# One PSUM bank for the two query-tile pairs of an attention step, three bias transposes in one tile, and four tiles of x loaded in head 14

## The chip, the cores and the metric

The kernel runs on one core of a Trainium2 chip. The metric is the device time of one execution in microseconds (us), lower is better. Three runs of the kernel before gave a median of 2459.82 us (2456.49 to 2463.15).

The engines are called as the profile calls them: PE is TensorE (matmuls; PEld is its loading of weights), DVE is VectorE, ACT is ScalarE, POOL is GpSimd, SP is SyncE, which here only issues DMAs. Each engine works through its own queue in order; semaphores tie the queues together. PSUM is the memory that PE writes into. [...]DVE and ACT read it.

## The reference

One block of a transformer with adaptive layer norm, all float32: 2048 tokens, model width 512.

```
mod = (silu(c) @ wmod)                      # sa, ca, ga, sb, cb, gb
h = layernorm(x) * (1 + ca) + sa
q = h Q_w + Q_b;  k = h K_w + K_b;  v = h V_w + V_b      # 16 heads of 128
scores = softmax(causal(q k^T / sqrt(128)))
x = x + ga * (concat_heads(scores v) O_w + O_b)
h = layernorm(x) * (1 + cb) + sb
x = x + gb * (experts(h) + shared(h))       # 64 experts of width 128, top 4; 2 shared of width 512
```

The change touches only the first half: the start (biases), the attention of the 16 heads, and the handing over to the output projection.

## The kernel before

**Start.** x is loaded in four blocks of 512 tokens, normalised on DVE (`norm_x`), transposed on PE (`turn_x`) and written by ACT, scaled, into `hT` (`place_x`). In between, at L375 to L379, the three bias matrices (16 heads x 128) are transposed on PE into PSUM tiles `bps` and copied by DVE into `qkb`. Each of the three has a tile of its own with the tag "po", of which there are two buffers. So the third transpose waits until DVE has copied the first.

**Attention.** For each head there are 16 query tiles of 128 rows, taken in pairs pr = 0 to 7 (256 query columns). Five steps s = 0 to 4 make a head:

```
BATCHES = ((7,), (6,), (5, 0), (4, 1), (3, 2))
```

Steps 0 and 1 hold one pair, steps 2, 3 and 4 two. The causal mask gives pair pr 2 pr + 2 key tiles. The loop at L736 runs over all 80 steps; in step n it weaves three streams of PE work together (`merge`, L83, which gives the streams turns in proportion to their columns):

- the softmax of step n + 2 (`softmax_tile`): scores by PE into `ps` (L497), the mask and the row maximum by DVE (L509, L510), exp by ACT (L516), and the division by the row sum, on DVE for s < 2 (L484), on ACT as `p<-p,rs` for the others (L704);
- the weighted values of step n (`weighted_values`): for each pair 2 pr + 2 matmuls into one PSUM tile `po` (L569), then one copy by ACT that adds the bias of V, `at<-po` (L578), then one DMA from POOL's queue that writes `at` to the DRAM tensor `atd` (L581);
- fillers: the projections of the next head's q and k (L217, steps 0 to 2) or the next pair of heads' v (L424, steps 3 and 4), and near the end the first output projections (`begin_output`, L678).

Between softmax and weighted values the probabilities must be transposed. After step n's streams `swap(n + 2)` issues 16 DMAs on SP that exchange blocks of 32 partitions from `p` to `pt` (L541, some 10 us of issue). One step later DVE transposes within the blocks, in two halves (`turn`, L551), at 0.55 and 0.8 of the step's columns. So a `po` matmul of step n + 2 needs both halves.

**Buffers that the change touches.** PSUM tiles with the tag "po" have two buffers of one bank each. A pair takes one, half filled (256 of 512 columns). The banks therefore rotate by pairs: 7, 6, 5, 0, 4, 1, 3, 2, and a pair waits until ACT has copied the pair two places before it. `at` has two buffers of 256 columns, and a copy into it waits until the DMA two places before has read it.

**The end of attention.** From head 14 on the weights of the output projection (`load_wo`), parts of `atd` (`load_ab`, L659), four tiles of x (`load_x_tile`, L668) and O_b (L770) are loaded by SP. Tiles 0 and 1 of x are loaded in head 14, step 4; tiles 2 and 3 in head 15, step 2, after `load_ab(2)`, four DMAs that make up 2 MB. All four tiles take buffers of the pool `ktp`, which otherwise holds the k of the heads (6 buffers); `qtp` does the same for q. `begin_output(t)` sums the heads 0 to 14 of token tile t on PE, then DVE adds the x tile (L688) and the bias (L689). At head 15, step 4, SP loads the first 512 tokens of head 15 from `atd` again (L783, L784); after the last step the pools of attention are given up, their memory is used by the next stage, and the output projection (L1027, L1048), the second layer norm (L862 to L873), routing and experts follow.

Of the kernel before, what the change touches and what calls it, by code (L numbers as in the profile page):

```python
# [9 lines left out]
F32 = mybir.dt.float32  # L10
BF16 = mybir.dt.bfloat16
U32 = mybir.dt.uint32
AF = mybir.ActivationFunctionType
ALU = mybir.AluOpType
# [4 lines left out]
P = 128  # L19
# [4 lines left out]
def adaln_block_kernel(  # L24
# [23 lines left out]
    nc = tc.nc  # L48
    _, N, D = x.shape
    H, _, DH = Q_w.shape  # L50
# [12 lines left out]
    scale = 1.0 / math.sqrt(DH)  # L63
# [4 lines left out]
    ident = const.tile([P, P], F32)  # L68
# [10 lines left out]
    atd = dram.tile([H, DH, N], F32)  # L79
# [39 lines left out]
    NE = 4  # L119
    parts = [silc.rearrange("p k n -> p (k n)")]  # L120
    with ExitStack() as att:
        enter = att.enter_context
# [139 lines left out]
        with tc.tile_pool(name="pre", bufs=1) as pre, tc.manual_schedule():  # L262
# [3 lines left out]
            b16s = []  # L266
# [62 lines left out]
            def norm_x(b):  # L329
                mv = pre.tile([P, 4, 2], F32, name="mv", bufs=2)  # L330
                for i in range(4):
                    st = pre.tile([P, 6], F32, name="st", bufs=4)
                    nc.vector.bn_stats(st, xs[b][:, i, :])
                    nc.vector.bn_aggr(mv[:, i, :], st)
                rstd = pre.tile([P, 4], F32, name="rstd", bufs=2)
                nc.scalar.activation(rstd, mv[:, :, 1], AF.Sqrt, bias=eps, scale=1.0)
                nc.vector.reciprocal(rstd, rstd)
                for i in range(4):
                    nc.vector.tensor_scalar(
                        xs[b][:, i, :], xs[b][:, i, :], mv[:, i, 0:1], rstd[:, i : i + 1],  # L340
                        ALU.subtract, ALU.mult,
                    )
# [29 lines left out]
            place_x(0, 0)  # L372
            place_x(0, 1)
            norm_x(1)
            for b in range(3):  # L375
                bps = psA.tile([P, H], F32, name="bps", tag="po")
                nc.tensor.transpose(bps, b16s[b], ident[:H, :H])
                nc.vector.tensor_scalar(qkb[:, b, :], bps, scale if b == 0 else 1.0, None, ALU.mult)
            nc.vector.tensor_sub(qkb[:, 3, :], qkb[:, 1, :], qkb[:, 0, :])  # L379
            for b in range(1, NB):  # L380
                for half in range(2):
# [13 lines left out]

        pp = enter(tc.tile_pool(name="pp", bufs=2))
        ptp = enter(tc.tile_pool(name="ptp", bufs=2))
        atp = enter(tc.tile_pool(name="atp", bufs=2))
        smp = enter(tc.tile_pool(name="smp", bufs=6))
        PW = 4 * (4 * NP - 1) * 32  # L400

# [151 lines left out]
        def weighted_values(hd, s, pt):  # L553

            g, hh = divmod(hd, HG)
            RB = blocks_of(s)
            rows = pt[:, : 4 * RB * 32].rearrange("k (a r q) -> k r a q", a=4, q=32)
            out = []
            for pr in BATCHES[s]:
                last = 2 * pr + 1  # L560
                box = []

                def one(kt, pr=pr, last=last, box=box):
                    if kt == 0:
                        box.append(psA.tile([P, 2 * P], F32, name="po", tag="po"))
                    po = box[0]
                    r = first_block(s, pr) + kt
                    wide = kt < last
                    nc.tensor.matmul(  # L569
                        out=po if wide else po[:, P:],  # L570
                        lhsT=vts[g, kt // 4][:, kt % 4, hh * DH : (hh + 1) * DH],
                        rhs=rows[:, r : r + last + 1 : last] if wide else rows[:, r + last],
                        start=(kt == 0),
                        stop=(kt == last),
                    )
                    if kt == last:
                        at = atp.tile([P, 2 * P], F32, name="at")
                        nc.scalar.activation(  # L578
                            at, po, AF.Identity, bias=qkb[:, 2, hd : hd + 1], scale=1.0
                        )  # L580
                        nc.gpsimd.dma_start(out=atd[hd, :, pr * 256 : (pr + 1) * 256], in_=at)  # L581

                for kt in range(last + 1):
                    out.append((256 if kt < last else 128, lambda kt=kt, one=one: one(kt)))
            return out
# [78 lines left out]
        xts = {}  # L664

        def load_x_tile(t):
            xts[t] = ktp.tile([P, 512], F32, name="kt")
            nc.sync.dma_start(out=xts[t], in_=x[0, t * P : (t + 1) * P, :])  # L668

        def begin_output(t):  # L670
# [54 lines left out]
        with tc.manual_schedule():  # L725
            work = softmax_work(0) + softmax_work(1)
            fill = [(1024, lambda t=t: make_v(0, t)) for t in range(NT)]
            fill += [(2048, lambda j=j: plain(0, j, qts[0, j])) for j in (2, 0, 1)]
            merge([work[:4], fill[:8]], [])
            swap(0)  # L730
            merge([work[4:], fill[8:]], [])
            swap(1)
            turn(0, 0)
            turn(0, 1)
            outs = []
            for n, (hd, s) in enumerate(steps):  # L736
                if s == 3:
                    if hd + 2 < H:
                        heads[hd + 2] = load_head(hd + 2)
                    if hd % HG == 1 and hd // HG + 2 < NG:  # L740
                        groups[hd // HG + 2] = load_group(hd // HG + 2)
                fill = fillers(hd, s)
                if (hd, s) in MOD_LOADS:
                    load_mod(MOD_LOADS[hd, s], hd // HG)
                if (hd, s) in MOD_ROWS:
                    fill.append((2048, lambda m=MOD_ROWS[hd, s]: late_mod(*m)))
                if (hd, s) in ((2, 3), (6, 3)):
                    mag = qkw.tile([P, 512], F32, name="p_")
                    gate(mag, ga if hd == 2 else gb)
                if (hd, s) == (14, 1):  # L750
                    fill.insert(2, (0, lambda: load_wo(0)))
                if (hd, s) == (14, 2):
                    load_wo(1)
                    load_ab(0, heads=((0, 4), (4, 8)))
                if (hd, s) == (14, 3):
                    load_wo(2)
                    load_ab(0, heads=((8, 12), (12, 14)))
                    first, second = [
                        vow.tile([P, DC, HG, DH], F32, name="wv").rearrange("p k i d -> p (k i d)")
                        for _ in range(2)  # L760
                    ]
                    parts += [first[:, :D], first[:, D:], second[:, :D]]
                    last3 = second[:, D : D + (NE - 1) * P]
                if (hd, s) == (14, 4):
                    load_wo(3)
                    load_ab(0, heads=((14, 15),))
                    load_x_tile(0)
                    load_x_tile(1)
                    rest = spare(hd // HG)
                    nc.sync.dma_start(out=rest[0][:, :D], in_=O_b.partition_broadcast(P))  # L770
                    for u in range(NE):
                        outs += begin_output(u)
                if hd == H - 1 and s == 0:
                    load_ab(1, heads=((0, 4), (4, 8)))
                if hd == H - 1 and s == 1:
                    load_ab(1, heads=((8, 12), (12, 15)))
                if hd == H - 1 and s == 2:
                    load_ab(2)
                    load_x_tile(2)
                    load_x_tile(3)  # L780
                if hd == H - 1 and s == 4:
                    nc.vector.tensor_copy(ga, rest[0][:, D:])
                    nc.sync.dma_start(out=last3, in_=atd[H - 1, :, : (NE - 1) * P])  # L783
                    nc.sync.dma_start(out=ones, in_=atd[H - 1, :, (NE - 1) * P : NE * P])  # L784
                if outs:
                    upto = 8 if hd < H - 1 else (14, 14, 14, 10)[s]
                    fill += outs[:upto]
                    del outs[:upto]
                streams = [weighted_values(hd, s, turned.pop(n)), fill]
                if n + 2 < len(steps):  # L790
                    streams.insert(0, softmax_work(n + 2))
                marks = [(f, lambda i=i: scale_wo(i)) for f, i in WO_SCALES.get((hd, s), ())]
                if s == 4 and hd + 2 < H:
                    marks.append((0.3, lambda: sum_w(hd + 2)))
                if n + 1 < len(steps):
                    marks.append((0.55, lambda: turn(n + 1, 0)))
                    marks.append((0.8, lambda: turn(n + 1, 1)))
                merge([st for st in streams if st], marks)
                if n + 2 < len(steps):
                    swap(n + 2)  # L800
            assert not outs and not ahead
# [676 lines left out]
```

## Time and profile before

| | us |
|---|---|
| median of three runs | 2459.82 |
| the profiled execution, its own time | 2473.66 |
| its span, first to last instruction | 2471.9 |
| mean granted PE clock | 0.991 of full |
| ACT copies `at<-po` L578 | 128 x 0.462 |
| POOL issues `atd<-at` L581 | 128, 0.627 each on average, 128 KB each |
| DVE copies of the biases L378 | 3 x 0.167 |
| ACT copy 128x512 from PSUM, L225 | 0.67 to 0.68 |

In the rows of groups of instructions the profile names the line, the engine, the operation and the tiles as output<-input, then the busy time and how long one takes. The bracket at the end of a row of the timeline is the time that the engine stood idle before the instruction, and what released it. A row of the waits reads "who <- for whom: us in total, times, longest". The clock column is the share of the full PE clock that was granted: 0.50 means that matmuls take twice as long. Times in the timeline count from the span's start.

The stages by the timeline: the first po matmul starts at 113.5 us, the last at 1729.5; a head takes about 100 us and a step about 20.

### The profile page before, as it was taken

What the parts mean: (1) busy time and instruction counts of PE and PEld (TensorE: products, weight loads), DVE (VectorE), ACT (ScalarE), POOL (GpSimd) and SP (SyncE); (2) the same over time, 40 slices, a digit from 0 to 9 for tenths busy, and PEclk for the clock granted to TensorE, in tenths of its full rate; (3) what the DMA queues carried; (4) which work ended last, traced back from release to release, by engine and by line L of the source; (5) the groups of instructions that cost most, each with busy time, mean ns of one, the idle gap of its engine ahead of it and who ended that gap; (6) DMA issues with size and microseconds to landing.
All of it is one profiled execution on the core that took longest, in us unless ns stands there. A gap on an engine that the chain in (4) does not pass through costs nothing. (4 is left out here: it accounts for less than half of the span.)

```text
span 2471.9 us, 26333 instructions
## 1 busy us (share of the span) xinstructions
PE 2376.8 (96%) x8406; PEld 1504.6 (61%) x8406; DVE 1512.2 (61%) x2878; ACT 838.1 (34%) x1785; POOL 224.1 (9%) x286
## 2 busy tenths in 40 slices
PE   7999999999999999999999999998999999999989
PEld 3656656566565665666656656555444476877734
DVE  5367666676666766667667676663655563644654
ACT  3244443443444434444344444432111222222200
POOL 0000000000000000000000000000000011111163
PEclk9999999999999999999999999999999999999989
DMA  4234444454354443444445444564432378778564
GB/s 137 62 79 113 116 118 106 97 135 107 94 133 104 101 119 91 111 111 104 116 96 122 105 103 118 161 174 128 152 119 85 102 206 249 230 212 252 171 190 133
DMA packets 223682, 325.23 MB, mean 132 GB/s; under 512 B 31876, under 2 KB 138424, under 8 KB 223544
## 3 DMA queue, kind: packets, MB, share of 16 engines
q1 hardware_dynamic: 196664, 252.21, 39.5%
q0 software_dynamic: 17664, 54.54, 7.3%
q10 hardware_dynamic: 9216, 16.78, 1.8%
q8 instruction: 68, 1.11, 0.2%
q14 instruction: 70, 0.57, 0.1%
HBM read 138.86 MB, written 41.94 MB: 73 GB/s over the span
## 5 line engine op out<-in xcount | busy, mean ns | idle before, releaser
L516 ACT ACTIVATE p<-ps,nm 128x1024 f32<-128x1024 f32 (+7 forms) x384 | 332.2, 865 | 897.0 <-DVE nm L514 411.5
L569 PE MATMUL po<-pt,v 128*128 128x256 f32 (+1 forms) x2304 | 575.5, 369 | 38.4 <-ACT at L578 33.4
L569 PEld LDWEIGHTS po<-pt,v 128*128 128x128 f32 x2304 | 426.5, 191 | 288.2 <-issue 190.5
L497 PE MATMUL ps<-kt,qt 128*128 128x512 f32 (+3 forms) x1280 | 531.2, 531 | 19.2 <-ACT p L516 16.8
L510 DVE TENSOR_REDUCE nm<-ps 128x1 f32<-128x1024 f32 (+7 forms) x384 | 348.8, 908 | 56.6 <-PE ps L497 47.8
L551 DVE STREAM_TRANSPOSE pt<-pt 128x1664 f32<-128x1664 f32 (+2 forms) x160 | 317.9, 1987 | 44.1 <-DMA pt<-p 40.5
L497 PEld LDWEIGHTS ps<-kt,qt 128*128 128x128 f32 x1280 | 234.7, 190 | 179.2 <-issue 137.0
L424 PE MATMUL pv<-wv,hT 128*128 128x256 f32 x1024 | 240.8, 379 | 2.2 <-ACT v L431 2.2
L581 POOL DMA_DIRECT2D atd<-at x128 | 80.1, 627 | 1649.4 <-ACT at L578 1111.7
L424 PEld LDWEIGHTS pv<-wv,hT 128*128 128x128 f32 x1024 | 194.4, 190 | 31.2 <-ACT v L431 3.0
L704 ACT ACTIVATE p<-p,rs 128x1024 f32<-128x1024 f32 (+7 forms) x256 | 200.0, 805 | 6.2 <-DVE rs L472 5.8
L509 DVE TENSOR_TENSOR ps<-ps,causal 128x128 f32<-128x128 f32 x256 | 74.1, 289 | 176.9 <-PE ps L497 174.5
L1048 PE MATMUL pso<-hT,T 128*128 128x512 f32 x384 | 175.6, 602 | 0.0
L217 PE MATMUL pqk<-T,sw 128*128 128x512 f32 x360 | 169.2, 592 | 0.0
L1340 PE MATMUL pse<-wgu,xbT 128*128 128x256 f32 x512 | 121.1, 379 | 0.0
L1048 PEld LDWEIGHTS pso<-hT,T 128*128 128x128 f32 x384 | 70.3, 193 | 72.1 <-issue 71.3
L217 PE MATMUL pqk<-hT,wq 128*128 128x512 f32 x240 | 113.7, 596 | 0.0
L1257 PE MATMUL psd<-wsd,hs 128*128 128x512 f32 x256 | 111.5, 592 | 0.0
L1340 PEld LDWEIGHTS pse<-wgu,xbT 128*128 128x128 f32 x512 | 93.8, 190 | 11.7 <-issue 1.0
L217 PEld LDWEIGHTS pqk<-T,sw 128*128 128x128 f32 x360 | 68.4, 190 | 47.7 <-issue 43.0
L1323 POOL DMA_INDIRECT xb<-h2d,tok x64 | 65.1, 1018 | 302.2 <-PE tpx L1333 273.0
L1335 ACT COPY xbT<-tpx 128x512 f32<-128x512 f32 x64 | 37.4, 586 | 145.7 <-DVE y L1363 58.0
(364 smaller groups left out, 2364.9 us busy)
## 6 DMA issues: line engine op xcount, KB each, us to landing
pt<-p SPq DMA_DIRECT2D x768, 104.0 KB
pt<-p SPq DMA_DIRECT2D x256, 124.0 KB
pt<-p SPq DMA_DIRECT2D x256, 108.0 KB
atd<-at POOLq DMA_DIRECT2D x128, 128.0 KB
wgu<-in_L_ffn_Wg_dram SPq DMA_DIRECT2D x64, 256.0 KB
wgu<-in_L_ffn_Wu_dram SPq DMA_DIRECT2D x64, 256.0 KB
wd<-in_L_ffn_Wd_dram SPq DMA_DIRECT2D x64, 256.0 KB
ybd<-y ACTq DMA_DIRECT2D x64, 256.0 KB
```

The lines of the kernel that those rows point to most:

```text
L217: nc.tensor.matmul(out=ps, lhsT=l[:, k], rhs=r[:, k], start=(k == 0), stop=(k == 1))
L424: nc.tensor.matmul(out=ps, lhsT=hTs[t // 4][:, k, (t % 4) * P : (t % 4 + 1) * P], rhs=wv[:, k].rearrange("p i d -> p (i d)"), start=(k == ...
L497: nc.tensor.matmul(out=ps[:, o : o + wo], lhsT=q, rhs=kts[hd, (c0 + o) // 512][:, :wo], start=True, stop=True,)
L510: nc.vector.tensor_reduce(nm[:, n : n + 1], ps[:, :w], AX.X, ALU.max, negate=True)
L516: nc.scalar.activation(rows[:, r0 + c0 // P : r0 + (c0 + w) // P], ps[:, :w].rearrange("q (r b k) -> q r b k", b=4, k=32), AF.Exp, bias=nm ...
L551: nc.vector.transpose(part, part)
L569: nc.tensor.matmul(out=po if wide else po[:, P:], lhsT=vts[g, kt // 4][:, kt % 4, hh * DH : (hh + 1) * DH], rhs=rows[:, r : r + last + 1 : ...
L581: nc.gpsimd.dma_start(out=atd[hd, :, pr * 256 : (pr + 1) * 256], in_=at)
L704: nc.scalar.activation(part, part, AF.Identity, scale=r)
L1048: nc.tensor.matmul(out=ps, lhsT=abs_[pr][:, hd, i * P : (i + 1) * P], rhs=wos[hd // 4][:, hd % 4, :], start=(hd == 0), stop=(hd == H - 1),)
L1257: nc.tensor.matmul(out=ps, lhsT=hsh[b, f][:, i * P : (i + 1) * P], rhs=wsd[:, f, :], start=(f == 0), stop=(f == NHC - 1),)
L1340: nc.tensor.matmul(out=ps, lhsT=xts[e][:, k, :], rhs=weights[e][:, k].rearrange("p i h -> p (i h)"), start=(k == 0), stop=(k == DC - 1),)
```

## The change

Three edits:

1. In `weighted_values` one PSUM tile `po` of a whole bank (2 x 256 columns) is taken per step. Pair n of the step accumulates into its half n. There is one ACT copy per step, after the last matmul of the last pair, of one or both halves; then one DMA per pair, in order. `at` becomes a single buffer of 2 x 256 columns; its size in memory is the same.
2. The three bias transposes write into one tile `bps`; the three copies by DVE come after all of them.
3. The four tiles of x are loaded together in head 14, step 4, before O_b. Tiles 2 and 3 take buffers of `qtp` instead of `ktp`. Nothing of x is loaded in head 15 any more.

```
+            bps = psA.tile([P, 3, H], F32, name="bps", tag="po")
             for b in range(3):
-                bps = psA.tile([P, H], F32, name="bps", tag="po")
-                nc.tensor.transpose(bps, b16s[b], ident[:H, :H])
-                nc.vector.tensor_scalar(qkb[:, b, :], bps, scale if b == 0 else 1.0, None, ALU.mult)
+                nc.tensor.transpose(bps[:, b], b16s[b], ident[:H, :H])
+            for b in range(3):
+                nc.vector.tensor_scalar(
+                    qkb[:, b, :], bps[:, b], scale if b == 0 else 1.0, None, ALU.mult
+                )
...
-        atp = enter(tc.tile_pool(name="atp", bufs=2))
+        atp = enter(tc.tile_pool(name="atp", bufs=1))
...
-            for pr in BATCHES[s]:
+            box = []
+            for n, pr in enumerate(BATCHES[s]):
                 last = 2 * pr + 1
-                box = []
-
-                def one(kt, pr=pr, last=last, box=box):
-                    if kt == 0:
-                        box.append(psA.tile([P, 2 * P], F32, name="po", tag="po"))
-                    po = box[0]
+
+                def one(kt, n=n, pr=pr, last=last):
+                    if not box:
+                        box.append(psA.tile([P, 2, 2 * P], F32, name="po", tag="po"))
+                    po = box[0][:, n]
...
-                    if kt == last:
-                        at = atp.tile([P, 2 * P], F32, name="at")
+                    if kt == last and n == len(BATCHES[s]) - 1:
+                        at = atp.tile([P, 2, 2 * P], F32, name="at")
                         nc.scalar.activation(
-                            at, po, AF.Identity, bias=qkb[:, 2, hd : hd + 1], scale=1.0
+                            at[:, : n + 1], box[0][:, : n + 1], AF.Identity,
+                            bias=qkb[:, 2, hd : hd + 1], scale=1.0,
                         )
-                        nc.gpsimd.dma_start(out=atd[hd, :, pr * 256 : (pr + 1) * 256], in_=at)
+                        for m, o in enumerate(BATCHES[s]):
+                            nc.gpsimd.dma_start(
+                                out=atd[hd, :, o * 256 : (o + 1) * 256], in_=at[:, m]
+                            )
...
         def load_x_tile(t):
-            xts[t] = ktp.tile([P, 512], F32, name="kt")
+            if t < 2:
+                xts[t] = ktp.tile([P, 512], F32, name="kt")
+            else:
+                xts[t] = qtp.tile([P, 512], F32, name="qt")
...
                 if (hd, s) == (14, 4):
...
-                    load_x_tile(0)
-                    load_x_tile(1)
+                    for u in range(NE):
+                        load_x_tile(u)
...
                 if hd == H - 1 and s == 2:
                     load_ab(2)
-                    load_x_tile(2)
-                    load_x_tile(3)
```

## The prediction on record

> **What bounds the kernel now.** I read the page's busy shares first, then the stages, then TensorE's (PE's) waits, and last the instructions around them. The first line below is from the page, the others from the windows view, cut before the first attention step, at its end, and around one late stall.
>
> ```profile
> PE 2376.8 (96%) x8406; PEld 1504.6 (61%) x8406; DVE 1512.2 (61%) x2878; ACT 838.1 (34%) x1785; POOL 224.1 (9%) x286
> ```
>
> ```profile
> 113.00:1735.00 1622.00, 1567.60 (x5446) 1008.31 (x5447) 1060.36 (x1843) 669.80 (x1416) 80.09 (x128) 1.00 0.46 114
> 1735.00:2472.00 737.00, 717.67 (x2633) 440.88 (x2631) 395.07 (x916) 131.29 (x300) 142.96 (x150) 0.98 0.57 175
> 1592.80:1596.20 3.40, 3.40 (x6) 1.68 (x6) 0.00 (x0) 1.86 (x4) 1.07 (x2) 0.50 0.55 153
> 1707.00:1712.20 5.20, 5.09 (x8) 2.86 (x9) 0.00 (x0) 1.14 (x3) 1.07 (x2) 0.50 0.57 150
> ```
>
> The columns are the stretch, its length, busy time of PE, PEld, DVE (VectorE), ACT (ScalarE) and POOL, then the granted PE clock. In the attention stage (113 to 1735) PE is busy 1567.6 of 1622 us; no other engine passes 66%. Time can be won only from PE's 54 idle us and from its slow-clock stretches. PE's waits in that stage:
>
> ```profile
> PE po L569 <- ACT at L578: 33.4, 16, 6.9
> PE ps L497 <- ACT p L516: 16.8, 16, 1.6
> PE po L569 <- DVE pt L551: 3.6, 1, 3.6
> ```
>
> Total us, times, longest. The first row is two thirds of it, once per head. The timeline shows where, in one head: PE first, then ACT.
>
> ```profile
> 477.98 1.88 PE L497 MATMUL ps<-kt,qt 128*128 128x512 f32 x4
> 481.68 0.70 PE L569 MATMUL po<-pt,v 128*128 128x256 f32 x2 [1.81 <-ACT at L578]
> ```
>
> ```profile
> 480.24 1.03 ACT L704 ACTIVATE p<-p,rs 128x896 f32<-128x896 f32 x1
> 481.17 0.83 ACT L578 ACTIVATE at<-po,qkb 128x256 f32<-128x256 f32 x2
> 481.88 0.83 ACT L704 ACTIVATE p<-p,rs 128x640 f32<-128x640 f32 x1
> ```
>
> This is the start of step s = 3. PE wants the po bank of pair 4. Two banks rotate pair by pair, so it is the bank of pair 5, from step s = 2, immediately before. Its 12 matmuls ended long ago, but its copy stands in ACT's queue beside that of pair 0, behind an exp and a scaling that themselves wait for the softmax. The other steps do not stall: their bank was copied well before.
>
> The one long stall is the last head's (6.86 us), and has another root, shown by DVE and PE:
>
> ```profile
> 1700.50 0.69 DVE L688 TENSOR_TENSOR wv<-psb,kt 128x512 f32<-128x512 f32 x1 [7.55 <-DMA kt<-in_L_attn_x_dram]
> 1701.22 0.69 DVE L689 TENSOR_TENSOR wv<-wv,v 128x512 f32<-128x512 f32 x1
> ```
>
> ```profile
> 1707.11 1.22 PE L569 MATMUL po<-pt,v 128*128 128x256 f32 x2 [6.86 <-ACT at L578]
> ```
>
> Tile 2 of x was issued at 1692.9 behind 2 MB of attention output (four loads at L659), and lands 7.5 us late. DVE stands, so do the softmax, ACT and the copy.
>
> **The change, part by part**, against the profiled execution (2473.66 us, span 2471.9); the plain runs' median, 2459.82, is 13.84 lower, and I subtract the same microseconds from it.
>
> *One bank per step.* Two buffers now rotate by steps, so a bank wanted by step n was copied at the end of step n-2, some 20 us before. In the changed kernel's instruction order the first po matmul of each step has indeed lost its wait for ACT and keeps those for the exchanged blocks (DMA) and their turning (DVE). What is late next at 479.86, where PE becomes free? The turning ended at 478.3; the two pv buffers were read by 476.5; the next score matmuls need a buffer whose exp ended at 480.2. Nothing stands within the 1.81 us. DVE follows a little less: the next turning starts at 490.85 bound by its DMA (0.22 us), whose issue hangs on ACT at 482.7 and comes only some 0.15 us earlier. DVE then keeps about 1.1 of the 1.8 us, but PE needs the second half at 500.97 and it ended at 498.6: 2.3 us of slack shrinks to 1.6. So PE keeps all. Sum: 33.4 - 6.86 = 26.5 us in 15 heads; the restart after each (0.70 for 0.59 us), 14 x 0.11 = 1.5; and head 14, whose 2.29 us stall is followed by 3.4 us at clock 0.50 (row above), half of it lost: 1.7. Together -29.7.
>
> On that last term the Trainium skill ("TensorE: Matmul & The Clock Gate", Part 1: the HAM clock gate) differs: it halves the clock after an idle window of about 3.4 us, and so a 2.29 us stall would cost nothing more. By the page -28.0, by the row -29.7; I take the row.
>
> *The rule that speaks against it.* The skill's "PSUM — Partial Sum Buffer" (PSUM bank collisions) says two engines may not be in one bank and partition quadrant at once. Pair one's copy can then not run under pair two's matmuls; were the bank wanted at once, 48 two-pair steps would each wait for copy and queue, about the 1.81 us of the row above: +87. By the trace the bank is wanted again some 20 us after its copy, so 0. I take 0.
>
> *ACT's copies.* 96 copies of 462 ns become 48 of 128x512; the nearest row (L225, same shape and source) takes 0.68 us: 48 x (0.92 - 0.68) = -11.5 us of ACT, which idles waiting for DVE. On the path 0.
>
> *One buffer of `at`.* Each copy now waits until the previous step's writes to DRAM have read the buffer. By the packets of POOL's queue a write lands 1.6 to 2.0 us after its issue, a handful 2 to 5.5. The next copy comes 19 us or more later: 0. Behind the copy stand the exps and the block exchange, so without that cover each microsecond of late landing would cost one per step. The writes stay 128, 0.54 us of POOL each, issued two together; POOL waits 1111.7 us for them, so 0.
>
> *Tiles of x in head 14.* Two 256 KB loads leave the place behind the 2 MB; two join SP's queue at 1627.5, ahead of O_b and of the exchange that starts at 1634.7. SP pays 2 x 0.6 us of issue inside its idle 5 us. DMA there is full until 1635.3 at about 310 KB/us: 0.5 MB add 1.7 us. O_b is wanted at 1639.5 and now lands by about 1637; the turning at 1643.7 already waits 0.22 us for the exchange. Between 0 and +2.5; I take +0.5, as the exchange has a quarter of the DMA free to catch up and PE had no idle there.
>
> *What it wins in head 15.* DVE goes on at 1692.9 instead of 1700.5. PE needs no copy at 1700.1, so it does 16.85 us of step s = 3 without the slow clock of 1707.1 to 1712.2 (2.6 lost): done at 1714.4. Next late is the turning for the last step: its scores end on PE at 1697.6, exp 6.1 us earlier than before, exchange issued at 1701.9 instead of 1708.16, second turning 11.8 us after that as now, ended at 1715.6. The last step starts there instead of at 1723.9: -8.2 (bounds -6.5 and -9.5).
>
> *Biases.* PE waits 5.54 us at 28.18 for the third transpose; the transposes of x behind it need the normalised rows, ready from 26.7 to 28.1. Gain 0 to 1; I take -0.8.
>
> *End of attention.* The last copy is 0.2 us longer, pair 3's write is issued together with pair 2's (+0.54) and joins a full DMA (+0.3). The last write, 6.06 us from issue to release, is on the chain (1730.6 to 1736.7, then DVE's normalisation, then PE idle 2.44 at 1750.2): +1.0 (0 to +1.5).
>
> Sum: -29.7 - 8.2 + 0.5 - 0.8 + 1.0 = -37.2. Profiled time 2436.5; plain runs 2459.8 - 37.2 = 2422.6, say 2423.
>
> **Rivals.**
> 1. The stall refills. For it: after PE's release DVE and the exchange gain less than PE; against: the slack above. If half of the 29.7 returns as waits for pt or scores: 2423 + 15 = 2438.
> 2. The wait isn't removed in effect: po's first matmul stands on pt instead, so only head 15, biases and end count (-7.5): 2452. Against: pt is done 1.6 us before PE arrives.
> 3. Slower: the single `at` buffer. If writes land after the next copy's turn, ACT stands, and exps and exchange behind it. It decides where landing nears 20 us; to eat the gain and 8 us more it must cost 45/79 = 0.57 us a step: 2468. Against: 1.7 us landings, even with the DMA at 46%.
> 4. The x loads delay the exchange by their full 2.5 us and the end costs 1.5: 2426, inside the first forecast.
>
> **How the numbers follow.** Forecast with rival 4: 0.74 (2415 to 2431); rival 1: 0.13; rival 2: 0.06; rival 3: 0.04; a small loss of unknown place: 0.03. The range reaches over rival 1: 2415 to 2445. 0.3% (7.4 us) is about what a measurement can tell from no change. Faster: the first two and most of rival 2, 0.92; same 0.04; slower 0.04.
>
> **What would show it.** The row "PE po <- ACT at" falls from 33.4 to under 2 us; `at` copies fall from 128 to 80 of 0.46 and 0.68 us; the clock stays 1.00 after the former 1592 and 1707; no DVE wait for x; the attention stage about 37 us shorter, the later stage within 2. Wrong if PE's waits for scores or pt grow by what the copies gave up, or if ACT waits for POOL's writes.

## The result, and the profile after

The changed kernel takes 2424.02 us, the median of four runs (2422.97 to 2424.49), against 2458.36 (2456.49 to 2463.15) for four runs of the kernel before. The ratio is 0.9858, with a 95% interval of 0.9844 to 0.9873: 34.3 us less. The forecast was 2423, in a range of 2415 to 2445. The profiled execution has an own time of 2422.97 us and a span of 2421.2. Before it were 2473.66 and 2471.9, so by the two profiles alone the gain is 50.7 us. Most of the other 16 us lie behind the part that was changed, where the prediction expected no difference; it is told below.

The page's first line, to be set beside that of before:

```profile
PE 2362.5 (98%) x8406; PEld 1500.5 (62%) x8406; DVE 1513.2 (62%) x2878; ACT 829.8 (34%) x1737; POOL 219.2 (9%) x286
```

PE has the same 8406 matmuls and is busy for 14 us less; ACT has 48 instructions fewer. The windows view, around the place of the former stall of head 14 and in the last step but one of head 15 (start:end, length, then PE, PEld, DVE, ACT and POOL busy, and the clock):

```profile
1562.00:1568.00 6.00, 6.00 (x19) 3.21 (x18) 3.39 (x8) 4.21 (x7) 1.07 (x2) 1.00 0.56 189
1671.00:1685.00 14.00, 12.95 (x45) 7.89 (x43) 3.56 (x2) 1.24 (x2) 1.07 (x2) 1.00 0.58 141
```

Both stood at 0.50 for a while in the profile of before. PE's waits from 60 to 1740 us:

```profile
PE ps L500 <- ACT p L519: 18.7, 18, 1.6
PE po L572 <- DVE pt L554: 5.2, 4, 3.6
PE pl L897 <- ACT h2T L889: 4.3, 1, 4.3
...
PE po L572 <- ACT at L581: 1.4, 1, 1.4
```

The row "po <- ACT at" was 33.4 us in 16 waits and is now one wait of 1.4, which belongs to the last step and is read below. The waits for scores grew only from 16.8 to 18.7, those for `pt` from 3.6 to 5.2. So the stall did not refill. That each head gives up its share is seen in one mark of every head, the score matmuls that wait for ACT near the end of its first step. The first head passes it 0.40 us earlier than before (135.21 for 135.61), the second 2.05, the third 4.12, and the fifteenth 26.83 (1522.97 for 1549.80), about 1.9 us a head.

The copies, in the answer about their line:

```profile
L581 ACT ACTIVATE at<-po,qkb x80: 452/674/690, 137.6 to 1691.3; 128x512 f32<-128x512 f32 x48, 128x256 f32<-128x256 f32 x32
```

The end of attention on DVE, then on PE:

```profile
1662.36 0.67 DVE L698 TENSOR_TENSOR wv<-psb,qt 128x512 f32<-128x512 f32 x1
...
1683.35 1.91 DVE L554 STREAM_TRANSPOSE pt<-pt 128x1664 f32<-128x1664 f32 x1 [3.20 <-DMA pt<-p]
...
1700.34 0.69 DVE L870 BATCH_NORM_STATS2 st<-acc 128x6 f32<-128x512 f32 x1 [3.67 <-DMA atd<-at]
```

```profile
1685.37 5.86 PE L572 MATMUL po<-pt,v 128*128 128x256 f32 x28 [1.41 <-ACT at L581]
...
1713.77 1.69 PE L897 MATMUL pl<-wr,h2T 128*128 128x64 f32 x8 [4.32 <-ACT h2T L889]
```

The first DVE row is the sum with tile 2 of x: it has no bracket, where DVE stood 7.55 us before. The last step starts at 1685.37. The bracket names ACT's copy, but ACT copied the bank of two steps earlier long before; what came last is the turning at 1683.35, which ends at 1685.26, 0.1 us before PE goes on. A wait for several semaphores must be read against the ends of all of them. The last DVE row waits 3.67 us for the final write of `at` (1.80 before), and so PE stands 4.32 us before `pl`, the routing matmul (2.44 before).

`pl` is a good place to cut the span in two. Its start moved from 1750.20 to 1713.77: 36.4 us by these two profiles, where 37.2 was forecast. The same code up to `pl` was profiled three more times below: before reached it at 1748.0 (e7_gather_lead), the changed kernel at 1715.5 and 1714.6 (r5_after, r11_after). So the gain up to `pl` is 32.5 to 36.4 us, on average 34.5, and 2 us of it can come or go between two executions of the same instructions. What follows `pl` should be untouched, but took 721.7 us in the profile of before and 707.4 in that of after.

### The profile page after: what moved, and what is told of

Its sections match the earlier page's. It is cut to its first block, busy times and chain, and to the rows that moved or that the text cites. A ratio compares the mean times of both kernels' runs of the same rounds, so it can differ in the third digit from the quotient of the medians.

```text
span 2421.2 us, 26178 instructions
## 1 busy us (share of the span) xinstructions
PE 2362.5 (98%) x8406; PEld 1500.5 (62%) x8406; DVE 1513.2 (62%) x2878; ACT 829.8 (34%) x1737; POOL 219.2 (9%) x286
## 5 line engine op out<-in xcount | busy, mean ns | idle before, releaser
L500 PE MATMUL ps<-kt,qt 128*128 128x512 f32 (+3 forms) x1280 | 531.2, 531 | 20.9 <-ACT p L519 18.7
L586 POOL DMA_DIRECT2D atd<-at x128 | 74.4, 584 | 1617.4 <-ACT at L581 1155.8
```

The source lines that it names most:

```text
L500: nc.tensor.matmul(out=ps[:, o : o + wo], lhsT=q, rhs=kts[hd, (c0 + o) // 512][:, :wo], start=True, stop=True,)
```

## The experiments

They came in three batches, each of which ran the kernel before again. Its medians were 2466.68 us (24 runs, 2460.08 to 2475.84) in the first, 2460.69 (17 runs, 2455.38 to 2465.97) in the second and 2457.28 (9 runs, 2450.74 to 2460.34) in the third. The theory was: one wait per head stood behind a copy that was late in ACT's queue, and the change removes it, with the late load of x as a second, separate cause. The rivals were: that the number of ACT's copies or the writes matter, or that the waits only move. "Up to pl" is the start of `pl` in the profiled execution; differences in it are taken from the profile of before, 1750.2, unless another is named. As the same code reached it 2 us apart, only differences clear of 2 us count there.

### First batch: each part alone, and the same effect by another means

**e1_x_tiles**: the kernel before with the third edit only.

```
         def load_x_tile(t):
-            xts[t] = ktp.tile([P, 512], F32, name="kt")
+            if t < 2:
+                xts[t] = ktp.tile([P, 512], F32, name="kt")
+            else:
+                xts[t] = qtp.tile([P, 512], F32, name="qt")
...
-                    load_x_tile(0)
-                    load_x_tile(1)
+                    for u in range(NE):
+                        load_x_tile(u)
...
-                    load_x_tile(2)
-                    load_x_tile(3)
```

> The kernel before with the third edit alone: tiles 2 and 3 of x loaded in head 14. My theory: DVE no longer waits 7.55 us for the tile, PE's stall at the last head's step 3 falls from 6.9 us to the 1.8 us of the other heads (the copy still stands in the way), and the slow clock behind it goes: 5 + 2.6 = 7.6 us, less what the turning of the last step gives back (1 to 2 us), so 5.5 to 7.6 us faster than before, about 2452. The fifteen other stalls stay at 26.5 us. Rival (the loads only move the collision to head 14's exchange): within 2 us of before, with DVE waits for pt of 3 us and more in head 15, step 0.

Measured: 2459.84 us (19 runs), ratio 0.9968 [0.9956, 0.9980], 6.8 us less, as expected; up to pl 1744.4, 5.8 less (3.6 by the second profile of before's code). PE's wait on the copies:

```profile
PE po L569 <- ACT at L578: 27.5, 16, 2.3
```

The times are still 16, but the longest is 2.3 where it was 6.9. The long stall of head 15 had the load as its cause, and the other 15 have another.

**e2_bank**: the kernel before with the first edit only (in the diff above, from `atp` down to the loop of DMAs).

> The kernel before with the first edit alone: one bank and one copy per step. My theory: 15 heads give back 29.7 us; in head 15 the wait for x stays, DVE's 7.55 us delay the last turning and the softmax, so PE gets past the po bank but then waits for the turned blocks of the last step; nearly all of the 8 us stay lost. The end of attention costs 2 us more. 27 to 30 us faster than before, about 2431. Rival (the gain is ACT's shorter work, 11.5 us): 11 us faster.

Measured: 2444.27 us (4 runs), ratio 0.9913 [0.9892, 0.9935], 22 less, where 27 to 30 were expected. Up to pl it is 1721.0, 29.2 less, as the theory has it, and PE's row `po <- ACT at` is gone. After pl it takes 721.5 us, like the profile of before. The runs of before in this batch spread over 16 us, so how far the missing 5 us or more lie in the later stage can't be told from the plain times.

**e3_order**: the kernel before, with the pairs of step 2 in the other order, 0 ahead of 5. Banks still rotate by pairs, and all 128 copies stay.

```
-            for pr in BATCHES[s]:
+            for pr in BATCHES[s][::-1] if s == 2 else BATCHES[s]:
```

> The kernel before with one line changed: in step s = 2 the weighted values of pair 0 come ahead of those of pair 5, so that the bank that step 3 wants first is that of pair 0, copied early in step 2. Still two half-filled banks that rotate by pairs, still 128 copies, x as before. My theory (what stalled PE was the place of one copy in ACT's queue when the bank is wanted): the fifteen stalls go as with the whole-bank edit, 27 to 31 us faster, about 2430, with 128 copies still there; the end of attention costs nothing more. Rival (the larger tile and the fewer copies are what helps): within 3 us of before.

Measured: 2437.08 us (4 runs), ratio 0.9884 [0.9862, 0.9906], 29.6 less; up to pl 1719.1, 31.1 less. PE's waits in attention and up to pl:

```profile
PE ps L497 <- ACT p L516: 19.2, 18, 2.5
PE po L569 <- DVE pt L551: 8.6, 3, 3.6
PE pl L889 <- ACT h2T L881: 2.4, 1, 2.4
```

The row "po <- ACT at" is gone, without one copy less and without a whole bank. With pair 0 first, its two matmuls' bank is the one that pair 4 wants, and it was copied early in the step. So the cause is the rotation of the banks against the place of the draining copy in ACT's queue, and neither the number nor the size of the copies. It also leaves the end of attention alone: PE's wait for `pl` stays at 2.4 us.

**e4_two_copies**: the changed kernel, whose full bank is copied by two instructions of 256 columns.

```
-                        nc.scalar.activation(
-                            at[:, : n + 1], box[0][:, : n + 1], AF.Identity,
-                            bias=qkb[:, 2, hd : hd + 1], scale=1.0,
-                        )
+                        for m in range(n + 1):
+                            nc.scalar.activation(
+                                at[:, m], box[0][:, m], AF.Identity,
+                                bias=qkb[:, 2, hd : hd + 1], scale=1.0,
+                            )
```

> The changed kernel, but the full bank copied by two copies of 256 columns at the end of the step instead of one of 512: ACT has 128 copies again, +11.5 us of its time. My theory (ACT's copies are off the path): within 2 us of the changed kernel, 2423 to 2426, about 35 us faster than before; ACT's busy time 11 us more. Rival (fewer copies are part of the gain): 2433 to 2436.

Measured: 2434.14 us (4 runs, 2433.33 to 2435.26), ratio 0.9872 [0.9852, 0.9893]. By the time alone the rival has won: it expected 2433 to 2436, and two copies seem to cost 10 us. The trace says otherwise. Up to pl it takes 1713.3 us, where the changed kernel takes 1713.8. All that it loses is behind pl, 718.9 us against 707.4, where nothing was edited. So it was run again in the third batch.

### Second batch: the end of attention, the remaining waits, and the later stage

**r5_after**: the changed kernel itself, to stand beside the next two.

> The changed kernel once more, unaltered, beside other kernels on one chip. The part of the gain up to the routing stage is fixed by the order of instructions: the last weighted-values matmul again some 38.5 us earlier than before. In the last stage (from the last expert matmul to the end) the profile of before lost 12.5 us that the profile of the changed kernel did not: DVE and ACT start 8 to 12 us after the PE result that they wait for. If that lag is a property of the changed order, it is absent in this profile too and the runs lie within 2 us of each other; if it comes and goes with the chip and the run, this profile or its runs show it: a spread of 8 us and more.

Measured: 2424.14 us (4 runs, 2423.28 to 2428.46), ratio 0.9859 [0.9840, 0.9878], 36.6 us less; up to pl 1715.5, then 706.6. The later stage lost nothing in the profile, but the runs spread over 5.2 us, where 2 or at least 8 were expected.

**e5_last_split**: the changed kernel, but the very last step (head 15, step 4) takes a bank and a copy per pair again.

```
-                    if not box:
+                    if not box or (kt == 0 and (hd, s) == (H - 1, NS - 1)):
+                        box.clear()
...
+                    if kt == last and (hd, s) == (H - 1, NS - 1):
+                        if n == 0:
+                            ats.append(atp.tile([P, 2, 2 * P], F32, name="at"))
+                        nc.scalar.activation(
+                            ats[0][:, n], po, AF.Identity,
+                            bias=qkb[:, 2, hd : hd + 1], scale=1.0,
+                        )
+                        nc.gpsimd.dma_start(
+                            out=atd[hd, :, pr * 256 : (pr + 1) * 256], in_=ats[0][:, n]
+                        )
-                    if kt == last and n == len(BATCHES[s]) - 1:
+                    elif kt == last and n == len(BATCHES[s]) - 1:
```

> The changed kernel, but in the very last step of attention pair 3 and pair 2 have a bank and a copy each, so that pair 3's write leaves before pair 2's matmuls end. My theory (the late write of both pairs is what DVE's first normalisation waits for): that wait for the write falls from 3.7 us to the 1.8 us of before, PE's idle at the first routing matmul from 4.3 to 2.4 us; 2 us faster than the changed kernel up to that point. Rival (the full DMA queues delay the write however early it is): unchanged, 3.7 and 4.3 us.

Measured: 2424.27 us (4 runs), ratio 0.9853 [0.9834, 0.9871]. PE's wait for `pl`, first of r5_after, then of this kernel:

```profile
PE pl L897 <- ACT h2T L889: 4.5, 1, 4.5
```

```profile
PE pl L909 <- ACT h2T L901: 2.4, 1, 2.4
```

From the start of the last step to `pl` this kernel takes 26.2 us, as before does; the profiles of the changed kernel take 28.3 to 28.6. So a bank, a copy and a write for each pair give back the 2 us at the end of attention, and that is shown. That it is the issuing of both writes together is not: e4_two_copies and its repetition below issue them together as well, each pair with its own short copy, and take only 26.8 to 27.0. In the plain times the 2 us can't be told from nothing here.

**e6_tile_order**: the changed kernel, in whose step 2 the last two softmax tiles change places. It is aimed at the row "ps <- ACT p", which the change leaves.

```
+            if s == 2:
+                return [(prs[0], 1), (prs[1], 1), (prs[1], 0), (prs[0], 0)]
             return [(prs[0], 1), (prs[1], 1), (prs[0], 0), (prs[1], 0)]
```

> The changed kernel, and in step s = 2 the softmax takes the first tile of pair 0 before that of pair 5: the narrow score tiles (256 and 128 wide) come one after the other instead of 384 and 128 last. This is the largest wait that PE keeps in attention (18.7 us, 1.0 to 1.6 us a head: the next step's first scores need the bank that the 384-wide exp still reads). Theory: it falls to under 5 us and the kernel is 14 to 18 us faster than the changed one. Rival: the wait moves to the place between the two narrow tiles and the next wide one, as two short exps in a row free a bank no sooner: within 3 us of the changed kernel.

Measured: 2419.45 us (5 runs, 2418.58 to 2420.67), ratio 0.9834 [0.9819, 0.9849], 4.7 below r5_after. The row of the waits is `ps <- ACT p` 14.4 us in 22 times, none over 0.8, where r5_after has 20.4. Neither expectation holds as written: the longest wait fell from 2.6 to 0.8, but waits came up at other tiles as well, and 6 of 20.4 us went. So the order of the tiles is not the main cause.

**e7_gather_lead**: the kernel before, whose last stage gathers the experts' rows two token tiles ahead instead of four. It is aimed at the later stage.

```
-            for t in order[:4]:
+            for t in order[:2]:
...
-                    if done + 4 < NT:
-                        got[order[done + 4]] = gather(order[done + 4])
+                    if done + 2 < NT:
+                        got[order[done + 2]] = gather(order[done + 2])
```

> The kernel before, with its attention untouched; in the last stage POOL's row gathers of the experts' results run two token tiles ahead of their use instead of four. Theory (DVE and ACT see PE's results late while POOL issues gathers without a pause): the lag of 8 to 12 us in the last stage goes, and the median is 6 to 12 us below before. Rival (the lag has nothing to do with the gathers): same as before within 3 us; or the gathers land too late for their use and it is slower.

Measured: 2456.74 us (12 runs), ratio 0.9987 [0.9978, 0.9997], 4.0 less, below the 6 to 12 that were expected. Its profiled execution takes 705.5 us after pl, without the delay that before's has (721.7). But r5_after, e5_last_split and e6_tile_order, in the same batch and with the longer lead, are without it too, and its own runs still spread over 8.8 us (2452.03 to 2460.79). Whether the gathers have to do with the delay, this run can't say.

### Third batch: the root of the waits for scores, and the repetition

**r11_after**: the changed kernel again, as the neighbour of the other three.

> The changed kernel, unaltered, as the measure for the three others on this chip: 34 to 38 us below before, no lag in its last stage.

Measured: 2425.40 us (4 runs), ratio 0.9871 [0.9855, 0.9887], 31.9 us less, below the 34 to 38 that were expected, as before is at 2457.28 in this batch; up to pl 1714.6, then 708.8.

**r10_two_copies**: e4_two_copies again.

> The kernel with two copies of 256 columns a step once more, now on the same chip as the changed kernel. If the extra copies cost nothing and its 10 us were the lag of the last stage on the other chip: within 3 us of the changed kernel here, or again 8 to 13 us slower with the lag of DVE and ACT behind PE seen in the last stage and nothing lost before it. If the copies cost: PE's waits in attention must be longer than the changed kernel's.

Measured: 2422.65 us (4 runs, 2421.07 to 2426.21), ratio 0.9865 [0.9848, 0.9882]; up to pl 1714.9, then 705.4. The same kernel took 2434.14 in the first batch, on a chip with the same number in the record (15), so "the other chip" of the expectation was a mistake. ACT is busy 835.1 us against 828.5 for r11_after, and the time is no longer: the second copy costs nothing that can be measured, and the 10 us of e4_two_copies were not its own. The rival fell.

**e8_cost**: the changed kernel, with another weight in the weaving. `merge` gives the streams turns by their columns. A narrow chunk of scores, 128 columns, counts little, so the next one comes a moment later and finds its `ps` buffer still unread by ACT. Here no chunk counts less than 512.

```
-            return [(min(SC, width - n * SC), lambda n=n: chunk(n)) for n in range(nch)]
+            return [
+                (max(512, min(SC, width - n * SC)), lambda n=n: chunk(n)) for n in range(nch)
+            ]
```

> The changed kernel, and a score tile narrower than 512 columns counts as 512 when PE's three streams are woven, so that more other matmuls stand between it and the next score tile. The order of the tiles is as in the changed kernel. Theory (PE waits for scores because the 384- and the 128-wide tiles of step s = 2 follow each other faster than DVE and ACT can free the bank): the 18.7 us of PE waiting for ACT's exp fall under 6 us, 12 to 16 us faster than the changed kernel, about 2410. Rival (the wait comes back at another tile, as in the reordered kernel): within 5 us of the changed kernel.

Measured: 2396.86 us (5 runs, 2395.09 to 2398.14), ratio 0.9758 [0.9745, 0.9772], 28.5 below r11_after. PE's waits of r11_after and of this kernel, then the first lines of their pages:

```profile
PE ps L500 <- ACT p L519: 19.2, 17, 2.0
```

```profile
PE ps L500 <- ACT p L519: 0.4, 1, 0.4
```

```profile
PE 2364.4 (98%) x8406; PEld 1501.1 (62%) x8406; DVE 1512.7 (62%) x2878; ACT 828.5 (34%) x1737; POOL 218.0 (9%) x286
```

```profile
PE 2355.9 (98%) x8406; PEld 1498.6 (63%) x8406; DVE 1506.8 (63%) x2878; ACT 824.5 (34%) x1737; POOL 218.1 (9%) x286
```

The wait is gone, which the theory wanted; but the gain is twice what was expected, since PE's busy time falls too, by 8.5 us. Up to pl the gain is 28.2: PE's idle time ahead of score matmuls falls by 20.3, and PE is busy for 7.9 us less in attention. The latter comes from how PE stops and starts again. At a stop, four score matmuls take 1.98 us where they take 1.88 elsewhere, and the last pair of matmuls ahead of it shows its end, some 0.17 us, which otherwise lies under the next. r11_after has thirty such places, two in each head but the last: one is the wait of 1.0 to 2.0 us, and the other so short, mostly 0.1 us, that the timeline prints no bracket:

```profile
733.52 1.98 PE L500 MATMUL ps<-kt,qt 128*128 128x512 f32 x4 [1.72 <-ACT p L519]
...
753.90 1.98 PE L500 MATMUL ps<-kt,qt 128*128 128x512 f32 x4
```

Thirty times 0.1 and 0.17 us are 8.1 us. In the trace, from one start to the next, the score matmuls lost 2.7 us and those into `po` 5.1, 7.8 together, so the whole is accounted for.

**e9_cost_split**: e8_cost and e5_last_split together.

> The same weaving, and in the last step of attention a bank and a copy for each pair. If both work as in the single runs, the sum of the two: 2 us below the kernel with the weaving alone, about 2408; PE's idle at the first routing matmul 2.4 us.

Measured: 2393.76 us (5 runs, 2392.70 to 2395.03), ratio 0.9745 [0.9731, 0.9758]; PE waits 2.4 us for `pl` where e8_cost waits 4.1. It is the fastest version of all, 3.1 us below e8_cost and 31.6 below r11_after.

## Why the prediction was right, step by step

The time came out 1 us from the forecast. Part of that is luck: 37.2 us were forecast as the gain and 34.3 came, and the median of before fell by 1.5 us with its fourth run. By stages, first from the profiles of before and after, then over all profiles of the same code (two of before up to `pl`, three of the changed kernel):

| step | forecast | before and after | all |
|---|---|---|---|
| one bank per step, with what the x loads cost in head 14 | -29.7 + 0.5 | -30.1 | -25.4 to -30.1 |
| head 15, up to the start of its last step | -8.2 | -8.1 | -8.1 to -8.2 |
| biases | -0.8 | -0.4 | -0.4 to -1.3 |
| end of attention | +1.0 | +2.2 | +2.0 to +2.4 |
| up to pl | -37.2 | -36.4 | -32.5 to -36.4 |
| after pl | 0 | -14.3 | |

- **One bank per step**: right. The end of head 15's step 2 moved from 1700.08 to 1669.58; without the biases' 0.4 that is -30.1. e2_bank has the same effect alone, and e3_order has it without the bank, so the named mechanism, the place of the copy in ACT's queue, is shown. "PE keeps all" held nearly: the rows for `pt` and scores together grew by 3.5 us in all, not by the 15 of rival 1.
- **The slow clock as part of the price**: true of the one profile, not of the kernel. The 2.29 us stall of head 14 stands in two more profiles, e7_gather_lead and e1_x_tiles, and no slow clock follows it there. In e7_gather_lead, by the timeline and then the windows view:

```profile
1591.98 0.70 PE L569 MATMUL po<-pt,v 128*128 128x256 f32 x2 [2.29 <-ACT at L578]
```

```profile
1592.20:1595.60 3.40, 3.40 (x10) 1.68 (x10) 0.00 (x0) 1.90 (x4) 1.07 (x2) 1.00 0.54 151
```

  So the row's 1.7 us are lost in one of three executions. The average over all profiles, -27.8, is nearer to -28.0 + 0.5 than to -29.7 + 0.5, though with such a spread it decides nothing. Taking the page's value would have been as good, and the 1.7 us came into the sum by the luck of one execution.
- **The rule that speaks against it** (+87 by the rule, 0 taken): right. PE shows no wait for a copy of its own step.
- **ACT's copies**: 11.5 us of ACT were forecast; 8.3 came (838.1 to 829.8), and r10_two_copies shows that they are worth nothing in time.
- **One buffer of `at`**: right as far as the trace shows it. ACT has no wait for a write of `at` in attention; the writes land 2.2 us after their issue (median; the longest takes 7.4). That two buffers would be no better was not tried.
- **Tiles of x**: right. DVE's 7.55 us are gone, and e1_x_tiles alone gives 5.8 up to pl. The price in head 14 can't be told from the first row of the table.
- **Head 15**: right, and what was next late is what was forecast, the turning for the last step.
- **Biases**: right in size, though one pair of profiles can't show it. The first po matmul starts at 113.08 instead of 113.49, but at 113.5 to 115.3 in the five profiles without the edit and at 113.0 to 114.0 in the nine with it, 0.8 earlier on average. The third transpose no longer stands; the next one waits 4.43 us for normalised rows instead.
- **End of attention**: the term that was mis-sized, +2.2 for +1.0. That the last write is on the chain was right, and e5_last_split takes the loss back. The copy and the issue were sized well: the last write leaves 0.8 us later, counted from the start of the last step. But it takes 7.4 us to land, and 6.0 in e7_gather_lead, whose end of attention is that of before (the profile of before itself has no landing times): 1.4 us more, where 0.3 was forecast. The wait at `pl` grows from 2.44 to 4.32. Why it lands later is open: in r10_two_copies both writes are issued together too, 0.2 us earlier, and the last one lands in 6.0.
- **"The later stage within 2"**: wrong for the profiles, which differ by 14.3 us there, and by this the profiled time of 2436.5 missed: it was 2422.97. The 13.84 us by which the profile of before stood above its median, which I only carried along, are close to these 14.3, so the plain runs of before lose less there than its profile. Not all lose nothing: in the third batch they go from 2460.34 at a mean granted clock of 0.993 to 2450.74 at 0.996, while the changed kernel's four lie within 3.5 us. So a few of the 34.3 us may belong to this delay and not to the change; the starts of `pl` say 32.5 to 36.4.

Taken together, the parts alone give -29.2 (e2_bank) and -5.8 (e1_x_tiles) up to pl, -35.0 of the -36.4, which is as near as one profile each can show. One sentence of the start was too narrow: time could be won not only from PE's idle and slow stretches, as e8_cost took 7.9 us from its busy time.

## What to carry to other kernels

When a wait names an engine that copies out of PSUM, ask which bank is wanted and where in that engine's queue the copy stands; reordering two pairs, in one line (e3_order), does nearly what the new layout does, and weighting a narrow chunk otherwise (e8_cost) takes off nearly as much again. Do not size a term by one profile, if another execution of the same code can be had. Cut the span at a mark behind the last edited instruction before you compare times: a kernel that loses its time where nothing was changed (e4_two_copies) has not been shown to be slower. Grouping the copies and writes at the very end of a stage cost 2 us here, so keep the last step ungrouped (e5_last_split by the trace; e9_cost_split by the time, 3.1 us).

## What the runs showed of the hardware that was not expected

**A delay in the last stage that comes and goes.** After pl, nine profiled executions took 705.4 to 709.1 us and five took 717.5 to 721.7, and nothing lies between. The five are those of the kernel before, e1, e2, e3 and e4; the nine are all others, among them r10_two_copies, the same kernel as e4_two_copies. So it isn't tied to the change. In the profiles it goes with the batch: all four of the first batch have it, and none of the eight of the two others, though the record names the same chip for the first and the third. In the profile of before it is in one place, DVE's addition of a shared expert's output (L1264), first in the kernel before, then in the changed kernel (L1272):

```profile
2380.10 0.69 DVE L1264 TENSOR_TENSOR acc<-acc,psd 128x512 f32<-128x512 f32 x1 [8.82 <-remote]
...
2392.09 0.69 DVE L1264 TENSOR_TENSOR acc<-acc,psd 128x512 f32<-128x512 f32 x1 [8.27 <-remote]
```

```profile
2332.82 0.69 DVE L1272 TENSOR_TENSOR acc<-acc,psd 128x512 f32<-128x512 f32 x1
2339.69 0.69 DVE L1272 TENSOR_TENSOR acc<-acc,psd 128x512 f32<-128x512 f32 x1 [3.10 <-PE psd L1265]
```

The changed kernel adds every 6.87 us, as PE delivers. In the kernel before PE's matmuls for them run in one unbroken stretch:

```profile
2349.36 27.63 PE L1257 MATMUL psd<-wsd,hs 128*128 128x512 f32 x64
```

It ends at 2377.0, a quarter of it every 6.9 us, yet DVE starts the last two additions 10 and 15 us after their matmuls; ACT, too, reads a finished `psg` 12 us late, and PE itself then stands. Through all of it POOL issues gathers without a pause, one every 1.3 us on average, and all go on at 2392, some 3 us after the last has been issued. But the changed kernel issues its gathers nearly as fast, one every 1.4 us from 2304.35 on, under the additions shown above, and has no delay; and most of the kernels without it have the longer lead too. So the gathers were only seen beside it, and why a finished matmul is seen so late is open.

**The clock after a stall.** In the profile of before the clock stood at 0.50 for 3.4 us behind PE's stall of 2.29 us, and while PE worked again behind the 6.86 us one for 5.2. The same stall of 2.29 us had no slow stretch behind it in e7_gather_lead, nor one of 2.30 in e1_x_tiles; a wait of 2.08 us had one in e2_bank (234.8 to 238.2 us), one of 2.75 in r10_two_copies had none. None of the 33 stalls of 1.81 us in the three profiles of before's attention had one. "TensorE: Matmul & The Clock Gate" (Part 1: the HAM clock gate) of the Trainium skill has an idle window of about 3.4 us; here shorter stalls were enough, but only in some executions. What decides it, no run here shows.
